# Cross attention in a transformer decoder: the shared table applied to four heads at once, and layer norm rows scaled by ScalarE

## The chip, the cores and the metric

The kernel runs on one core of one Trainium2 chip. The metric is device time in microseconds, from the start to the end of one execution; less is better. A core has five engines that run side by side, each with its own queue of instructions: PE (TensorE, matrix multiplications), DVE (VectorE), ACT (ScalarE), POOL (GpSimd) and SP (SyncE, which here issues DMA transfers). They wait for each other on semaphores.

## The reference

A two-layer decoder on x of 8 batches, 512 rows (positions) and 256 columns. Layer 0 has a self attention, a cross attention with 16 heads and a local transformer; layer 1 an integer attention, a media attention and a mixture of experts. The change lies in layer 0's cross attention and in the layer norms just before and behind it. Cut to what matters:

```python
def _layernorm(x, axis=-1, eps=1e-05):
    m = jnp.mean(x, axis=axis, keepdims=True)
    v = jnp.var(x, axis=axis, keepdims=True)
    return (x - m) / jnp.sqrt(v + eps)
...
        scores = scores + adj[None, None, :, :]
        scores = jnp.where(mask == 0, jnp.float32(-jnp.inf), scores)
        weights = jax.nn.softmax(scores, axis=-1)
```

The queries come from the layer norm of x, the keys and values from a context of 512 rows for each batch. `adj` is one table of 512x512 for all batches and heads, `mask` one of 512x512 for each batch and all heads. The result of the cross attention is added to x; the local transformer starts from the layer norm of the sum.

## The kernel before, in words

Everything here is float32. `FastDecoder` runs the stages one after the other; x lies in SBUF as 8 batches of 4 tiles of 128 rows by 256 columns.

**Table.** Since exp(s + a) = exp(s)·exp(a), the kernel takes the exponential of `adj` once, and for each batch multiplies it by (mask != 0) into `x_share` (L1608: four tiles of 128 keys by 512 queries). A step then needs the exponential of the scores times a tile of that table.

**Steps.** The stage's loop has 128 steps, 16 for each batch: four groups of four heads, each over four tiles of 128 keys. Step n does three things:
- `scores(n)`: four matmuls on four row groups of PE (L1720), which write two PSUM tiles `sc` of 128 x (2 heads x 512 queries), from a ring of three such tiles.
- `soften(n)`: for each of the two tiles an exponential on ACT into an SBUF tile `x_e` (L1731, ring of six), and a multiplication of it by the shared tile on DVE (L1732). The shared tile is broadcast over the two heads.
- `weigh(n-2)`: four matmuls that weigh the values with the multiplied exponentials of two steps before (L1748), summed over the four key tiles in one PSUM bank `po`. After the fourth key tile ACT copies `po` to `x_o` (L1754). Sums, a DMA, a reciprocal on DVE (L3248) and a multiplication on POOL (L1765) follow.

PE's order in a step is scores(n), weigh(n-2), then the extra matmuls.

**Work spread between the steps.** While one batch is in its 16 steps, `prepare` makes the next one's operands, a few pieces for each step: the keys (PE L1638, evacuated by ACT into `x_k`, L1653), `x_xn`, the normalised rows of x (L1614, through `normalize`, a DVE instruction for each tile of 128x256, L157), transposes (L1630, ACT L1633), queries (L1638 again, ACT `x_q` L1646), values (L1658, ACT `x_v` L1662), the table (L1608), and on POOL the addition of a bias to x once `x_xn` has been taken (L1619). These matmuls share one PSUM bank, `pj`, which ACT or DVE must have emptied before the next writes it.

The batch that ended before is finished in the same steps through a list `later` with delays in steps: output projections (PE L1781) and their addition to x on DVE (L1786) with the statistics for the next layer norm (L1491, L1492), a DMA that saves x to `away` (L1793), an estimate of the reciprocal root (L1495 to L1497) with three Newton rounds (L1502 to L1504) one step apart, and, from the fifth step on, the scaling of the four tiles of x in place, two to a step (`normal`, L1507, through `normalize`, L157; in the profile these are `x<-x,lt_ln_mean,lt_ln_rstd`).

**What sets the order.** A scheduler lays out each engine's queue by the program's order and priorities, and adds the semaphores. `paced` (L1703) puts a piece behind DVE's multiplication of the step before last, kept in `marks`; it only orders, and waits for nothing else. The mean and reciprocal root for `x_xn` of all batches are worked out in the self attention before, by `means` (L1419), and copied to `x_ln_mean` and `x_ln_rstd`; the first batch is prepared there too. In the last 12 steps the local transformer's first matmuls (L1885) are drawn in between.

Of the kernel before, what the change touches and what calls it, by code (L numbers as in the profile page):

```python
# [27 lines left out]
F32 = mybir.dt.float32  # L28
# [5 lines left out]
AF = mybir.ActivationFunctionType  # L34
ALU = mybir.AluOpType
# [4 lines left out]
P = 128  # L40
B, S, C = 8, 512, 256
NST = S // P
NT = B * NST
# [1234 lines left out]
class FastDecoder(Decoder):  # L1278
# [31 lines left out]
    def stage_self_attention(self, w, ahead):  # L1310
# [3 lines left out]
        nc = self.nc  # L1314
# [3 lines left out]
        with self.tc.tile_pool(reuse_waits="tile", name="sa", bufs=2) as pool, self.tc.tile_pool(  # L1318
# [4 lines left out]
            shift = self.alloc(pool, [P, 1], F32, "sa_shift", bufs=1)  # L1323
# [24 lines left out]
            def norm(b):  # L1348
                d = held[b] = {"h": hs[b % 2]}
                x = self.x[:, b * NST : (b + 1) * NST, :]  # L1350
                stats = self.ln_stats(pool, lambda i: [x[:, i, :]], NST, "sa_ln")
                d["xn"] = self.alloc(pool, [P, NST, C], F32, "sa_xn", bufs=3)
                for i in range(NST):
                    self.normalize(d["xn"][:, i, :], x[:, i, :], stats, i)
# [64 lines left out]
            def means(b):  # L1419

                x = self.x[:, b * NST : (b + 1) * NST, :]
                at = slice(b * NST, (b + 1) * NST)
                for kept, new in zip(self.x_ln, self.ln_stats(pool, lambda i: [x[:, i, :]], NST, "x_ln")):
                    nc.vector.tensor_copy(kept[:, at], new)

            self.x_ln = [self.alloc(self.const, [P, NT], F32, "x_ln_" + n) for n in ("mean", "rstd")]
            norm(0)
            norm(1)
            weights()
# [3 lines left out]
            for b in range(B):  # L1433
                scores(b)
                if b + 1 < B:
                    turn(b + 1)
                    project(b + 1)
                    values(b + 1)
                weigh(b)
                if b + 2 < B:  # L1440
                    norm(b + 2)
                if b > 0:
                    means(b - 1)
                    ahead.step(3)
# [24 lines left out]
    def rsqrt(self, pool, out, v, tag):  # L1469
# [4 lines left out]
        for _ in range(3):  # L1474
            nc.vector.scalar_tensor_tensor(t, out, -0.5, out, ALU.mult, ALU.mult)  # L1475
            nc.vector.tensor_tensor(t, t, v, ALU.mult)
            nc.vector.scalar_tensor_tensor(out, t, 1.5, out, ALU.add, ALU.mult)

    def ln_pieces(self, pool, rows, out, tag):


        nc = self.nc
        mv = self.alloc(pool, [P, NST, 2], F32, tag + "_mv")
        mean = self.alloc(pool, [P, NST], F32, tag + "_mean")
        var = self.alloc(pool, [P, NST], F32, tag + "_var")
        rstd = self.alloc(pool, [P, NST], F32, tag + "_rstd")
        t = self.alloc(pool, [P, NST], F32, tag + "_t")

        def stats(i):
            st = self.alloc(pool, [P, 1, 6], F32, tag + "_bn", bufs=4)  # L1490
            nc.vector.bn_stats(st[:, 0, :], rows[:, i, :])  # L1491
            nc.vector.bn_aggr(mv[:, i, :], st.rearrange("p a b -> p (a b)"))  # L1492

        def guess():
            nc.vector.tensor_copy(mean, mv[:, :, 0])  # L1495
            nc.vector.tensor_scalar(var, mv[:, :, 1], EPS, None, ALU.add)
            nc.vector.tensor_scalar(  # L1497
                rstd.bitcast(I32), var.bitcast(I32), -0.5, float(0x5F3759DF), ALU.mult, ALU.add
            )

        def newton():
            nc.vector.scalar_tensor_tensor(t, rstd, -0.5, rstd, ALU.mult, ALU.mult)  # L1502
            nc.vector.tensor_tensor(t, t, var, ALU.mult)
            nc.vector.scalar_tensor_tensor(rstd, t, 1.5, rstd, ALU.add, ALU.mult)  # L1504

        def normal(i):
            self.normalize(out(i), rows[:, i, :], (mean, rstd), i)  # L1507

        return (
            [lambda i=i: stats(i) for i in range(NST)], [guess] + [newton] * 3,  # L1510
            [lambda i=i: normal(i) for i in range(NST)],
        )

# [10 lines left out]
    def stage_cross_attention(self, ahead):  # L1524
# [6 lines left out]
        nc, t = self.nc, self.t  # L1531
# [7 lines left out]
        pool = first  # L1539
# [33 lines left out]
        bias = self.alloc(pool, [P, C], F32, "x_bias", bufs=1)  # L1573
# [14 lines left out]
        def prepare(b):  # L1588

            d = held[b] = {"v": v_pad[b % 2]}  # L1590
# [14 lines left out]
            def share(k):  # L1605
# [5 lines left out]

            x = self.x[:, b * NST : (b + 1) * NST, :]
            normals = [
                lambda i=i: self.normalize(d["xn"][:, i, :], x[:, i, :], self.x_ln, b * NST + i)  # L1614
                for i in range(NST)
            ]

# [75 lines left out]
        with self.tc.tile_pool(reuse_waits="tile", name="xa", bufs=2) as pool, self.tc.tile_pool(  # L1693
# [7 lines left out]
            marks = []  # L1701

            def paced(thunk):  # L1703

                with self.tc.issue_after(marks[-2]):
                    thunk()

            def scores(n):
# [16 lines left out]
            def soften(n):  # L1725
                b, rest = divmod(n, 16)
                kt = rest % 4
                d = held[b]
                for p in range(2):
                    ex = self.alloc(pool, [P, 2, 512], F32, "x_e", bufs=6)  # L1730
                    nc.scalar.activation(ex, d["e"][rest][p], AF.Exp)  # L1731
                    nc.vector.tensor_tensor(  # L1732
                        ex, ex, d["share"][:, kt, :].unsqueeze(1).broadcast_to([P, 2, 512]), ALU.mult
                    )
                    d["e"][rest][p] = ex
                marks.append(self.newest(mybir.EngineType.DVE))

            def weigh(n):
                b, rest = divmod(n, 16)
                G, kt = divmod(rest, 4)  # L1740
                g, e = divmod(G, 2)
                d = held[b]
                if kt == 0:
                    d["po"] = self.alloc(psum, [P, 512], F32, "po")
                ex = d["e"].pop(rest)
                for m in self.together(4):
                    r = (m + 2) % 4
                    nc.tensor.matmul(  # L1748
                        d["po"][32 * r : 32 * r + 32, :], d["v"][:, kt, 8 * g + 2 * r + e, :],
                        ex[r // 2][:, r % 2, :], start=(kt == 0), stop=(kt == 3),  # L1750
                    )
                if kt == 3:
                    o = self.alloc(pool, [P, S], F32, "x_o", bufs=3)
                    nc.scalar.copy(o, d["po"])  # L1754

                    if e == 0:
                        d["oT", g] = self.alloc(pool, [P, S], F32, "x_oT", bufs=5)
                        d["wide", g] = self.alloc(pool, [P, S], F32, "x_wide")
                    oT, wide = d["oT", g], d["wide", g]
                    at = [slice(32 * r + 16 * e, 32 * r + 16 * e + 16) for r in range(4)]  # L1760
                    for r in range(4):
                        nc.sync.dma_start(oT[at[r], :], o[32 * r + 1 : 32 * r + 17, :])

                    def multiply():
                        nc.gpsimd.tensor_tensor(oT, oT, wide, ALU.mult)  # L1765
                        if g == 1:
                            for i in range(NST):
                                later.add(3 + i, lambda i=i: project_out(b, i))

                    def divide(rows):  # L1770
                        for r in range(4):
                            nc.sync.dma_start(wide[at[r], :], rows[r : r + 1, :].broadcast_to([16, S]))
                        if e == 1:
                            later.add(2, multiply)

                    self.inverted(pool, o[0:P:32, :], later, divide)

            def project_out(b, i):
                ps = self.pj()
                for g in range(2):  # L1780
                    nc.tensor.matmul(  # L1781
                        ps[:, :C], held[b]["oT", g][:, i * P : (i + 1) * P], wo[:, g, :],
                        start=(g == 0), stop=(g == 1),
                    )
                x = self.x[:, b * NST + i, :]
                nc.vector.tensor_tensor(x, x, ps[:, :C], ALU.add)  # L1786
                if i == 0:
                    rows = self.x[:, b * NST : (b + 1) * NST, :]
                    held[b]["norm"] = self.ln_pieces(pool, rows, lambda i: rows[:, i, :], "lt_ln")
                means, roots, normals = held[b]["norm"]  # L1790
                means[i]()
                if i == NST - 1:
                    nc.sync.dma_start(self.away[b], self.x[:, b * NST : (b + 1) * NST, :])  # L1793
                    for k, root in enumerate(roots):
                        later.add(1 + k, lambda root=root: paced(root))
                    for k, normal in enumerate(normals):
                        later.add(5 + k // 2, lambda normal=normal: paced(normal))

            n = 16 * B
# [1719 lines left out]
```

## Time and profile before

| | |
|---|---|
| median of 3 runs | 3094.61 us (3087.45 to 3096.63) |
| profiled execution | 3094.66 us |
| its span, first to last instruction | 3092.7 us |
| mean granted TensorE clock | 0.974 |
| PE busy in the span | 2842.4 us (92%) |
| DVE busy | 2158.3 us (70%) |
| ACT busy | 1155.1 us (37%) |
| POOL busy | 409.6 us (13%) |

The cross attention's steps run from about 205 to 664 us of the span. In the profile's rows, `L1732 DVE TENSOR_TENSOR x_e<-x_e,x_share 128x1024` is DVE's instruction of line 1732, its output and inputs, and the shape in partitions by elements; then come the count, the busy time in all and the mean in ns of one, and the idle time of the engine just before such instructions, with the one that ended it. In rows of the timeline the first two numbers are the start and the length in us. PEld is PE's loading of weights, which overlaps its matmuls. Busy times of a pipelined engine overlap a little from one instruction to the next: two multiplications of 1.2 us start 1.13 us apart.

### The profile page before, as it was taken

To read this page: it belongs to the slowest core of one execution; us is meant where nothing else is said; L and a number is where in the kernel's file an instruction comes from. 1 tells how busy PE (TensorE), PEld (TensorE's weight loads), DVE (VectorE), ACT (ScalarE), POOL (GpSimd) and SP (SyncE) were. 2 spreads that over 40 slices of the span, in tenths; PEclk is the share of its full clock that TensorE was granted. 3 is DMA by queue.
4 is the path that set the end of the run, shared out by engine and by line. 5 is a ranking of instruction groups with operands and counts; after the bars stand their busy time and mean duration, and the time that the engine had idled before them with its cause. 6 is when DMAs were issued, how large, how long until landed. Compare 5 with 4: busy or idle time off the path is not lost. (4 is left out here: it accounts for less than half of the span.)

```text
span 3092.7 us, 40203 instructions
## 1 busy us (share of the span) xinstructions
PE 2842.4 (92%) x14929; PEld 1507.6 (49%) x14944; DVE 2158.3 (70%) x4962; ACT 1155.1 (37%) x1623; POOL 409.6 (13%) x389
## 2 busy tenths in 40 slices
PE   8999999969999999999999999999786999997998
PEld 5653333225555556555555556555344334434665
DVE  7458999977887894357887898548788766665110
ACT  2237777724334321124344331115263443441111
POOL 1111111100001010000101111112111123231111
PEclk9999999989999999999999999999997999998999
DMA  7011212101001001001000012010332122223231
GB/s 242 1 35 50 71 49 70 36 19 56 15 15 29 15 24 36 0 1 43 22 15 22 22 38 69 14 41 28 125 122 76 52 93 83 90 69 96 98 139 61
DMA packets 130696, 168.74 MB, mean 55 GB/s; under 512 B 51760, under 2 KB 79665, under 8 KB 128442
## 3 DMA queue, kind: packets, MB, share of 16 engines
q1 hardware_dynamic: 126394, 154.48, 16.0%
q0 software_dynamic: 4096, 11.59, 1.0%
q8 instruction: 119, 1.95, 0.3%
q14 instruction: 87, 0.71, 0.1%
HBM read 113.12 MB, written 47.50 MB: 52 GB/s over the span
## 5 line engine op out<-in xcount | busy, mean ns | idle before, releaser
L1885 PE MATMUL pj<-w,la_hT 128*128 128x512 f32 x720 | 342.8, 615 | 32.7 <-DVE x L2062 16.3
L1732 DVE TENSOR_TENSOR x_e<-x_e,x_share 128x1024 f32<-128x1024 f32 x256 | 317.6, 1283 | 16.7 <-ACT x_e L1731 16.5
L1731 ACT ACTIVATE x_e<-sc 128x1024 f32<-128x1024 f32 x256 | 249.4, 1023 | 82.0 <-PE sc L1720 82.0
L1885 PEld LDWEIGHTS pj<-w,la_hT 128*128 128x128 f32 x720 | 131.7, 194 | 189.3 <-issue 118.1
L2007 ACT ACTIVATE la_e<-la_e 128x1024 f32<-128x1024 f32 (+1 forms) x128 | 121.1, 952 | 209.2 <-DVE la_e L2003 209.2
L2890 ACT ACTIVATE ma_e<-sc,ma_bias 128x1024 f32<-128x1024 f32 x128 | 135.8, 1110 | 165.3 <-PE sc L2884 165.3
L2216 ACT ACTIVATE lf_gate<-pj,lf_b 128x512 f32<-128x512 f32 (+1 forms) x82 | 56.3, 687 | 346.6 <-PE pj L2195 337.2
L2897 DVE TENSOR_TENSOR ma_esum<-ma_esum,ma_e 128x1024 f32<-128x1024 f32 x96 | 129.8, 1353 | 71.3 <-ACT ma_e L2890 34.8
L2195 PE MATMUL pj<-lf_hnT,w 128*128 128x512 f32 (+1 forms) x368 | 171.7, 595 | 0.6 <-DVE lf_hid L2221 0.6
L2003 DVE TENSOR_TENSOR la_e<-sc,la_mask 128x1024 f32<-128x1024 f32 (+1 forms) x128 | 137.0, 1081 | 41.1 <-PE sc L1995 41.0
L3262 POOL TENSOR_TENSOR la_oT<-la_o,x_wide 128x512 f32<-128x512 f32 x64 | 88.3, 1387 | 571.0 <-DMA x_wide<-invs 315.4
L1748 PE MATMUL po<-x_e,x_v 128*32 128x512 f32 x1024 | 138.1, 612 | 21.9 <-DVE x_e L1732 15.2
L2195 PE MATMUL sc<-lf_hnT,w 128*128 128x512 f32 x336 | 157.9, 592 | 0.0
L1720 PE MATMUL sc<-x_q,x_k 32*128 32x512 f32 x1024 | 151.3, 640 | 1.7 <-DVE sa_ok L1448 1.4
L2267 PE MATMUL po<-w,lf_hid 128*128 128x256 f32 x640 | 148.8, 379 | 0.0
L2221 DVE SCALAR_TENSOR_TENSOR lf_hid<-sc,lf_b,lf_gate 128x512 f32<-128x512 f32 x70 | 52.4, 748 | 126.9 <-PE sc L2195 126.9
L1995 PE MATMUL sc<-la_qkT 64*128 64x256 f32 (+1 forms) x1024 | 124.2, 373 | 12.3 <-ACT la_qkT L1931 11.3
L1892 ACT ACTIVATE la_sq<-pj 128x512 f32<-128x512 f32 x120 | 71.4, 595 | 170.3 <-PE pj L1885 170.3
L2057 PE MATMUL pj<-w,la_oT 128*128 128x256 f32 x512 | 122.3, 385 | 11.3 <-DVE x L2062 9.4
L2884 PE MATMUL sc<-ma_qT,ma_kT 64*128 64x512 f32 x512 | 129.9, 626 | 0.0
L2267 PEld LDWEIGHTS po<-w,lf_hid 128*128 128x128 f32 x640 | 117.8, 190 | 20.2 <-issue 6.7
L2908 PE MATMUL po<-ma_e,ma_v 128*64 128x512 f32 x512 | 124.2, 606 | 0.0
(493 smaller groups left out, 5296.2 us busy)
## 6 DMA issues: line engine op xcount, KB each, us to landing
x_wide<-invs SPq DMA_DIRECT2D x184, 128.0 KB
w<-in_f_w_dram SPq DMA_DIRECT2D x16, 1024.0 KB
kv<-kv_o SPq DMA_DIRECT2D x56, 256.0 KB
slots<-x_empty SPq DMA_DIRECT2D x8, 1028.0 KB
x_mask<-in_x_maskT_dram SPq DMA_DIRECT2D x8, 1024.0 KB
ma_kT<-kv SPq DMA_DIRECT2D x8, 1024.0 KB
ma_v<-kv SPq DMA_DIRECT2D x8, 1024.0 KB
ex_rows<-slots SPq DMA_DIRECT2D x7, 1028.0 KB
```

Of the source, the lines that this page charges most:

```text
L1720: nc.tensor.matmul(pair[r // 2][:, r % 2, :], d["k"][rows, g, kt * P : (kt + 1) * P], d["q"][rows, e, g, :], start=True, stop=True,)
L1731: nc.scalar.activation(ex, d["e"][rest][p], AF.Exp)
L1732: nc.vector.tensor_tensor(ex, ex, d["share"][:, kt, :].unsqueeze(1).broadcast_to([P, 2, 512]), ALU.mult)
L1748: nc.tensor.matmul(d["po"][32 * r : 32 * r + 32, :], d["v"][:, kt, 8 * g + 2 * r + e, :], ex[r // 2][:, r % 2, :], start=(kt == 0), stop=( ...
L1885: nc.tensor.matmul(ps, d["hT"][:, k, i * P : (i + 1) * P], wqkv[:, k, j * S : (j + 1) * S], start=(k == 0), stop=(k == 1),)
L1995: nc.tensor.matmul(both[half][:, r, jj * 256 : jj * 256 + to - j * P], d["qkT"][rows, 4 + c, j * P : (j + 1) * P], d["qkT"][rows, c, j * P ...
L2003: nc.vector.tensor_tensor(ex[:, :, :n_cols], ps[:, :, :n_cols], mask[:, :n_cols].unsqueeze(1).broadcast_to([P, 2, n_cols]), ALU.add,)
L2195: nc.tensor.matmul(ps[:m, :], w1[:, k, at : at + m], held[b]["hnT"][:, k, :], start=(k == 0), stop=(k == 1))
L2267: nc.tensor.matmul(ps[:, :C], held[b]["hid"][:, f, i * P : (i + 1) * P], w2[:, f, :], start=(f == 0), stop=False,)
L2884: nc.tensor.matmul(both[m // 2][:, r, :], d["k"][rows, c, kt * P : (kt + 1) * P], d["q"][rows, c, :], start=True, stop=True,)
L2890: nc.scalar.activation(ex, ps, AF.Exp, bias=bias[:, b * NST + kt : b * NST + kt + 1], scale=0.125)
L2897: nc.vector.tensor_tensor(d["sum", c], d["sum", c], ex, ALU.add)
```

## The change

Three edits.

1. `soften` takes one tile `x_e` of 128 x (4 heads x 512), from a ring of three, in place of two of half the size from a ring of six. The two exponentials write its halves, and one multiplication of 128x2048 by the shared tile, broadcast over four heads, follows both. `weigh` reads the four heads from it. `marks` keeps the newest DVE and the newest ACT instruction of each step, and `paced` puts its piece behind both.
2. The scaling of rows goes from `normalize` (DVE, `(x - mean) * rstd`) to `on_scalar`, an ACT activation of kind Identity with a bias and a scale for each row: `x * rstd + shift`. That holds for `x_xn` (32 tiles over all batches) and for the rows of x behind the cross attention (32 tiles).
3. The shift, -mean·rstd, is made by DVE: in `means` by an instruction that takes the place of a copy, and in `ln_pieces` by one more 128x4 instruction in the last Newton round (`last`), once for each batch.

```diff
@@ means, in the self attention
-                for kept, new in zip(self.x_ln, self.ln_stats(pool, lambda i: [x[:, i, :]], NST, "x_ln")):
-                    nc.vector.tensor_copy(kept[:, at], new)
+                mean, rstd = self.ln_stats(pool, lambda i: [x[:, i, :]], NST, "x_ln")
+                shift, scale = self.x_ln
+                nc.vector.scalar_tensor_tensor(shift[:, at], mean, -1.0, rstd, ALU.mult, ALU.mult)
+                nc.vector.tensor_copy(scale[:, at], rstd)
@@
+    def on_scalar(self, out, in_, stats, i):
+        shift, scale = stats
+        self.nc.scalar.activation(
+            out, in_, AF.Identity, bias=shift[:, i : i + 1], scale=scale[:, i : i + 1]
+        )
@@ ln_pieces
+        def last():
+            newton()
+            nc.vector.scalar_tensor_tensor(mean, mean, -1.0, rstd, ALU.mult, ALU.mult)
+
         def normal(i):
-            self.normalize(out(i), rows[:, i, :], (mean, rstd), i)
+            self.on_scalar(out(i), rows[:, i, :], (mean, rstd), i)
...
-            [lambda i=i: stats(i) for i in range(NST)], [guess] + [newton] * 3,
+            [lambda i=i: stats(i) for i in range(NST)], [guess, newton, newton, last],
@@ prepare
-                lambda i=i: self.normalize(d["xn"][:, i, :], x[:, i, :], self.x_ln, b * NST + i)
+                lambda i=i: self.on_scalar(d["xn"][:, i, :], x[:, i, :], self.x_ln, b * NST + i)
@@ paced
-                with self.tc.issue_after(marks[-2]):
+                with self.tc.issue_after(marks[-2][0]), self.tc.issue_after(marks[-2][1]):
@@ soften
+                ex = self.alloc(pool, [P, 4, 512], F32, "x_e", bufs=3)
                 for p in range(2):
-                    ex = self.alloc(pool, [P, 2, 512], F32, "x_e", bufs=6)
-                    nc.scalar.activation(ex, d["e"][rest][p], AF.Exp)
-                    nc.vector.tensor_tensor(
-                        ex, ex, d["share"][:, kt, :].unsqueeze(1).broadcast_to([P, 2, 512]), ALU.mult
-                    )
-                    d["e"][rest][p] = ex
-                marks.append(self.newest(mybir.EngineType.DVE))
+                    nc.scalar.activation(ex[:, 2 * p : 2 * p + 2, :], d["e"][rest][p], AF.Exp)
+                nc.vector.tensor_tensor(
+                    ex, ex, d["share"][:, kt, :].unsqueeze(1).broadcast_to([P, 4, 512]), ALU.mult
+                )
+                d["e"][rest] = ex
+                marks.append([self.newest(e) for e in (mybir.EngineType.DVE, mybir.EngineType.Activation)])
@@ weigh
-                        ex[r // 2][:, r % 2, :], start=(kt == 0), stop=(kt == 3),
+                        ex[:, r, :], start=(kt == 0), stop=(kt == 3),
```

## The prediction, made before the result was known

> **What bounds the kernel now.** I read the costliest groups first, then busy time in a window, then the waits, then the timeline of one batch. Groups:
>
> ```profile
> L1732 DVE TENSOR_TENSOR x_e<-x_e,x_share 128x1024 f32<-128x1024 f32 x256 | 317.6, 1283 | 16.7 <-ACT x_e L1731 16.5
> L1731 ACT ACTIVATE x_e<-sc 128x1024 f32<-128x1024 f32 x256 | 249.4, 1023 | 82.0 <-PE sc L1720 82.0
> ```
>
> The multiplication is VectorE's dearest group and was let wait only 16.7 us. Windows (length, then PE, PEld, DVE, ACT, POOL busy, clock, DMA, GB/s): one whole batch, then the stage:
>
> ```profile
> 416.00:470.00 54.00, 51.21 (x313) 17.11 (x312) 51.06 (x73) 39.58 (x50) 8.11 (x3) 1.00 0.21 61
> 205.00:664.00 459.00, 417.06 (x2473) 135.13 (x2469) 420.83 (x601) 317.37 (x389) 56.71 (x27) 0.97 0.17 48
> ```
>
> A batch repeats every 53.9 us. PE and DVE are both 95% busy; ACT has a quarter free. Who waits for whom, over the stage (total, times, longest):
>
> ```profile
> PEld po L1748 <- DVE x_e L1732: 37.6, 42, 2.0
> PE po L1748 <- DVE x_e L1732: 15.2, 17, 3.7
> ```
>
> PE itself lost only 15.2 us to the multiplication (in most of the weight loads' 37.6 PE was still busy with the matmuls before). PE's own sum for a batch, from starts in the timeline: scores 1.07 + weighing 1.00, 16 times, 33.1; keys and queries 4x1.92 = 7.7; values 4x1.06; transposes 2x0.58; output projections 4x1.06; together 50.5. So 3.4 us of 53.9 is stall: **PE's issue order bounds the stage, and DVE is just behind it.** The two stretches of timeline where that decides, ACT, then DVE (start, length, what, idle before):
>
> ```profile
> 428.82 1.94 ACT L1731 ACTIVATE x_e<-sc 128x1024 f32<-128x1024 f32 x2 [0.44 <-PE sc L1720]
> 432.47 0.69 ACT L1653 ACTIVATE x_k<-pj,x_bk 128x512 f32<-128x512 f32 x1 [1.70 <-PE pj L1638]
> 433.57 1.94 ACT L1731 ACTIVATE x_e<-sc 128x1024 f32<-128x1024 f32 x2 [0.41 <-PE sc L1720]
> ```
>
> ```profile
> 429.68 2.35 DVE L1732 TENSOR_TENSOR x_e<-x_e,x_share 128x1024 f32<-128x1024 f32 x2
> 431.95 0.15 DVE L1502 SCALAR_TENSOR_TENSOR lt_ln_t<-lt_ln_rstd 128x4 f32<-128x4 f32 x1
> 432.14 0.16 DVE L1503 TENSOR_TENSOR lt_ln_t<-lt_ln_t,lt_ln_var 128x4 f32<-128x4 f32 x1
> 432.34 0.16 DVE L1504 SCALAR_TENSOR_TENSOR lt_ln_rstd<-lt_ln_t,lt_ln_rstd 128x4 f32<-128x4 f32 x1
> 432.42 2.35 DVE L1732 TENSOR_TENSOR x_e<-x_e,x_share 128x1024 f32<-128x1024 f32 x2
> 434.69 0.73 DVE L157 TENSOR_SCALAR x<-x,lt_ln_mean,lt_ln_rstd 128x256 f32<-128x256 f32 x2
> ```
>
> The exponentials from 428.82 are step 34's, the multiplication of step 34 starts at 432.42: DVE lags ACT by a whole step, and the last Newton round, which the row scaling needs, ends at 432.42.
>
> **The Trainium skill.** "VectorE: DVE Perf Modes", section "The TRN2 errata — SBUF-src ops pay a fixed extra latency per instruction": an fp32 two-tensor operation costs (N+151)/0.96 ns: 1224 at 1024, 691 at 512; the trace's median is 1216 (la_r, 128x512: 685), so it agrees. "ScalarE: Activation LUTs", section "What ACT_TABLE_LOAD costs": 186+0.833N ns with immediates, some 93 more for each [128,1] pointer operand, 93 of overlap back to back: 799 for x_q (512, two pointers), measured 773; near enough. "SBUF — State Buffer", section "SBUF: two separate sides": a two-tensor DVE operation and a GpSimd one lock each other out for a whole instruction; the mean 1283 over the median 1216, up to 3409, fits. "PSUM — Partial Sum Buffer", section "Engine vs sequencer instructions": an engine's queue is strictly first in, first out.
>
> **The change, part by part.**
>
> *Wide multiplication.* By extrapolation 1216 + 2x(1216-685) = 2278 ns (page: 2291). Starts show two halves 2.27 apart back to back with what follows; one wide costs about 2.2: 0.07 us of DVE pitch a step, 9 us over 128. Against it, the first half may start only when the second exponential is done, 1.0 us later, but a step's weights are used two steps later. In light steps (2.27 us apart) exponentials ending at 425.40 plus 2.3 give 427.7, and the weighing two steps on would come at about 427.68: no slack, no gain. I book nothing: the scores and extra matmuls that PE issues between hide it, and 0.2 us a light step (one without key, query or value matmuls; about 6 a batch, 7 batches, +8) is the cost if that cover is gone.
>
> *Removed from DVE.* 28 L157 at 612 ns (16.0 us) and 24 at 406 (8.8), 24.8 us in the stage window. They stood after the multiplications of steps 35 to 38, where PE, bound by keys and values, didn't wait. Gain on the path: 0. Eight extra 128x4 operations at 0.16 us: 1.3 us, 0.17 of it ahead of the scaling each time.
>
> *Added to ACT.* A 128x256 activation with two pointers isn't in the trace. Nearest: 773 - 256x0.833 = 560 ns (page, estimate: 585), pitch 0.46; bounds 0.40 (x_v, 403, no pointers) and 0.65. 64 x 0.46 = 30 us of ACT, which has 14 us a batch free. Work isn't the question, place is: by ACT's program order the first two scalings of lt rows stand between step 34's two exponentials. The last Newton round stands in DVE's queue after step 33's multiplication. The first exponential of step 34 ends about 429.84; the shift is ready at 432.42 + 0.17 = 432.6 less a little wide-multiply gain, say 432.45. ACT waits 2.6 us there, and queued behind it are the exponential, the key evacuation (so pj), and all later steps. From 432.45 ACT is one chain to the next po evacuation: four pairs of scalings at 0.93 (3.7), seven exponentials at 0.94 (6.6), two x_k at 0.6 (1.2), x_o 0.5: 12.0. The weighing of step 36, which needs po, starts at 444.6 to 444.7, where before:
>
> ```profile
> 442.81 1.06 PE L1748 MATMUL po<-x_e,x_v 128*32 128x512 f32 x8
> ```
>
> That is 1.9 us late, and the rest of the batch is PE's own work, which recovers nothing. The same DVE rows stand at 324.15 and 485.61 in other batches. Five batches have both lt rows and preparation: +9.5. Two have only the x_xn scalings, half an exponential pair each: +0.45, +0.9. The sixth lt batch, beside no preparation, stalled already for 1.76 before weighing at 601.14: +0.1. In sum +10.5.
>
> *Self-attention.* The first four x_xn scalings stand on ACT between exponentials of the second image; they wait for rstd and shift (ready about 50.4), and exponentials due at 48.65 and 50.37 and the copy of sa_xnT (50.95) queue behind, so the projection at 51.58 comes some 2.2 later: +2.2.
>
> *Tail of the stage, 601 to 664.* PE waits 10.13 and 4.18 us for DVE's la_v copies, which queue behind multiplications that now come whole, later by about 0.85 each: +1.8 (0 to 3).
>
> *Start of the local layers.* The last normals waited on DVE for the saving DMA, which landed at 704.27 (idle 4.83). Now ACT waits for it, with la_sq and la_qk behind it in its queue, where DVE had nothing pressing: +1.5 (0 to 2).
>
> POOL's bias addition (L1619) waited 42.3 us for x_xn from DVE and will wait for ACT instead, a little later; its reader is the output projection's addition to x more than twenty steps on, so 0. SP's and POOL's orders don't move; no DMA is added, but x's normals now reach SP's saving transfer from another engine: it reads x before they write, so it isn't later. Sum 10.5 + 2.2 + 1.8 + 1.5 = 16. The profiled execution took 3094.66 (span 3092.7, 2 outside), level with the median 3094.61: **3110 us**.
>
> **Rivals.**
>
> *B, covered.* ACT's wait is swallowed by PE's slack (sc has three buffers, weights two steps) and by the 3.4 us of stalls: about 3095. For: a quarter of ACT is free. Against: 12.0 us of unbroken chain after the wait.
>
> *C, faster.* DVE's relief ends its one-step lag. PE's waits for DVE at steps 30 to 34 (0.95 and 0.69 us in this batch) and 0.33 later vanish: 1.6x6 + 0.33x7 = 12, so about 3083. All that PE lost to DVE here, 15.2 (x_e) + 4.1 (lt_ln_t) + 3.5 (x L1786) = 23, bounds it at 3072. It decides if the shift is ready before step 34's first exponential ends, 2.6 us sooner than now. Against: the lag is made by a DMA wait (reciprocal at 424.10, idle 0.81) and by added rows before the scalings' place, and neither changes.
>
> *D, slower still.* As forecast, and the wide multiplication has no slack in light steps (+8), with GpSimd locking it out as a whole near L1619 (5 us, +3): about 3121.
>
> **How the numbers follow.** Chances: forecast 0.46, B 0.16, C 0.22, D 0.16. What a measurement of this kernel can tell from no change is about 0.3%, 9.3 us: below 3085.3 is faster, above 3103.9 slower. The forecast's own range is 3104 to 3118 (activation at 0.40 or 0.65: 8 scalings x 5 batches x up to 0.15 is 6 either way, tail and start 3). C straddles 3085 and D is wholly slower, so faster 0.20, same 0.18, slower 0.62. The range from 3084 to 3121 leaves out half of C and half of D.
>
> **What the profile after would show.** Right: 128 rows of 128x2048 at about 2.28; 64 ACT rows 128x256 at about 0.56; before the first lt scaling of each batch ACT idle about 2.6 us, released by DVE; a batch at about 55.8 us where both kinds stand, and PE's waits for ACT grown. Wrong: ACT idle there under 1 us and a batch at 52 to 53 (C), a batch at 53.9 (B), a multiplication at 2.4 or more with PE waiting for it in light steps (D). What would undo the forecast is DVE being ahead at step 33, so that nothing in ACT's queue waits, or an activation far from 0.56.

## The result: slower by 1%, and where the time went

The changed kernel took 3124.87 us (median of 4 runs, 3118.12 to 3126.87) against 3091.31 us for the kernel before beside it (4 runs, 3087.45 to 3096.63): a ratio of 1.0099, 95% interval 1.008 to 1.0118. The forecast was slower, 3110 us, at most 3121: the sign and the main mechanism were right, the size too small by almost half. The profiled execution has a span of 3120.8 us, 28.1 more than before.

Groups of the page after:

```profile
L1744 DVE TENSOR_TENSOR x_e<-x_e,x_share 128x2048 f32<-128x2048 f32 x128 | 304.6, 2394 | 68.4 <-ACT x_e L1743 68.4
L1743 ACT ACTIVATE x_e<-sc 128x1024 f32<-128x1024 f32 x256 | 250.0, 1024 | 71.5 <-PE sc L1732 66.2
```

DVE spends 13 us less on the multiplication (317.6 before) and idles 68.4 us before it for ACT, where it was 16.7. Busy time in the same two windows as before (length; PE, PEld, DVE, ACT, POOL; clock, DMA, GB/s):

```profile
416.00:470.00 54.00, 49.78 (x309) 16.11 (x302) 45.46 (x49) 40.99 (x55) 6.09 (x3) 1.00 0.19 60
205.00:664.00 459.00, 408.77 (x2401) 130.07 (x2399) 372.94 (x409) 329.20 (x428) 54.20 (x27) 0.97 0.16 47
```

DVE is relieved as meant, but by less than the 420.8 and 372.9 us of the window say, because the last four of the 128 steps now lie behind it: from the start of step 0 to that of step 127 DVE was busy for 409.8 us before and 378.2 after. PE, which sets the pace, did 2437 matmuls between these two starts in both kernels, in 445.5 us before and 464.9 after. The waits of the stage, 205 to 664 us (who, for whom: total, times, longest):

```profile
DVE x_e L1744 <- ACT x_e L1743: 63.4, 47, 4.5
PEld po L1760 <- DVE x_e L1744: 36.2, 27, 4.0
PEld po L1760 <- ACT x_o L1766: 20.9, 19, 1.4
PE po L1760 <- DVE x_e L1744: 20.4, 15, 3.7
ACT x L1483 <- DVE lt_ln_mean L1516: 12.3, 5, 2.8
```

The last row is the new wait that the forecast named: five times, up to 2.8 us. Where the span's 28.1 us arose is read from the starts of the first exponential of each step (ACT's rows are complete), after less before, and further on from the first lf_gate activation (of the local transformer's feed-forward part, at 1125 us before; la_ names belong to its attention):

| stretch | forecast, us | measured, us |
|---|---|---|
| up to step 0 (self attention) | 2.2 | 1.75 |
| steps 0 to 32 | 0.9 | 1.85 |
| steps 32 to 112 (five batches with lt scalings and preparation) | 9.5 | 16.2 |
| steps 112 to 127 (sixth lt batch and tail) | 1.9 | 1.45 |
| step 127 to the first lf_gate | 1.5 | 7.6 |
| the rest | 0 | -0.65 |
| sum | 16 | 28.1 |

**One of the five batches, as the timeline has it after** (ACT, DVE, POOL and PE, each asked by itself; start, length, what, idle before). It is the batch shown before, with its step 64 now 9.63 us later:

```profile
438.19 1.02 ACT L1743 ACTIVATE x_e<-sc 128x1024 f32<-128x1024 f32 x1 [0.45 <-PE sc L1732]
442.05 1.09 ACT L1483 ACTIVATE x<-x,lt_ln_mean,lt_ln_rstd 128x256 f32<-128x256 f32 x2 [2.83 <-DVE lt_ln_mean L1516]
443.05 1.00 ACT L1743 ACTIVATE x_e<-sc 128x1024 f32<-128x1024 f32 x1
```

```profile
441.81 0.16 DVE L1516 SCALAR_TENSOR_TENSOR lt_ln_mean<-lt_ln_mean,lt_ln_rstd 128x4 f32<-128x4 f32 x1
444.08 2.29 DVE L1744 TENSOR_TENSOR x_e<-x_e,x_share 128x2048 f32<-128x2048 f32 x1 [2.11 <-ACT x_e L1743]
...
453.68 6.68 DVE L1744 TENSOR_TENSOR x_e<-x_e,x_share 128x2048 f32<-128x2048 f32 x2 [1.12 <-ACT x_e L1743]
```

```profile
453.64 2.36 POOL L1631 TENSOR_TENSOR x<-x,x_bias 128x1024 f32<-128x1024 f32 x1
```

```profile
454.17 1.07 PE L1760 MATMUL po<-x_e,x_v 128*32 128x512 f32 x8 [0.35 <-ACT x_o L1766]
...
458.21 1.06 PE L1760 MATMUL po<-x_e,x_v 128*32 128x512 f32 x8 [0.84 <-DVE x_e L1744]
```

The two scalings stand between the exponentials of 438.19 and 443.05, which are one step's. ACT idles 2.83 us, then DVE idles 2.11 us, because the wide multiplication needs the second exponential. The weighing that needs po starts at 454.17; it was 442.81, so less the 9.63 it is 1.73 late: the 1.9 of the forecast. (The prediction calls the steps of this batch's scalings 34 to 38; by the count of the stage's 128 steps they are 66 to 70. Its sum doesn't rest on the number.) What the forecast lacked is the next weighing, which waited 0.84 us for DVE: two wide multiplications took 6.68 us where 4.5 is usual, while POOL's bias addition ran. Before, four halves took about as long, but DVE had started them in time (POOL, DVE):

```profile
445.39 5.05 POOL L1619 TENSOR_TENSOR x<-x,x_bias 128x1024 f32<-128x1024 f32 x1 [3.47 <-DVE x_xn L157]
```

```profile
448.27 6.66 DVE L1732 TENSOR_TENSOR x_e<-x_e,x_share 128x1024 f32<-128x1024 f32 x4
```

**Some three of the 28 us follow a late transfer.** Batch 5 (steps 80 to 96) alone lost 5.9 us, the other four between 1.9 and 3.1 (in a second profile of this kernel 4.9, and 2.7 to 4.1). In it the reciprocal of the sums waited 2.89 us for a DMA (0.50 before), PE waited 3.13, and then ran at half clock (window's columns as above; DVE, PE, then the window):

```profile
492.35 0.25 DVE L3260 RECIPROCAL x_inv<-x_sums 128x16 f32<-128x16 f32 x1 [2.89 <-DMA x_sums<-sums]
```

```profile
494.81 1.94 PE L1760 MATMUL po<-x_e,x_v 128*32 128x512 f32 x8 [3.13 <-DVE x_e L1744]
```

```profile
495.00:500.00 5.00, 5.00 (x24) 0.73 (x18) 4.90 (x8) 1.61 (x2) 0.00 (x0) 0.50 0.16 43
```

The eight matmuls took 1.94 us, 1.06 at full clock. The late transfer is not the change's alone: of five profiles of the kernel before, one (before_d, below) has a wait of 2.56 us for it too, and lost 2.2 us in that batch; the other four wait 0.26 to 0.50.

**The start of the local layers.** Not the scalings made it late: ACT's last ones waited only 0.23 us for the saving DMA, and wide_only (below), which has them on DVE, lost 9.4 us in this stretch. PE's clock did. Between step 127 and the first of the last eight output projections, half clock stood for 14.2 us where it was 6.8 before, and 3.6 us were lost; two groups of four matmuls took some 3.4 us each, 1.98 before. One of them, before and then after:

```profile
669.79 1.98 PE L1885 MATMUL pj<-w,la_hT 128*128 128x512 f32 x4 [0.68 <-ACT la_qkT L1931]
```

```profile
692.63 3.46 PE L1897 MATMUL pj<-w,la_hT 128*128 128x512 f32 x4 [0.68 <-ACT la_qkT L1943]
```

Then the eight projections ran at half clock. The second of them, before and then after:

```profile
683.21 1.13 PE L1781 MATMUL pj<-w,x_oT 128*128 128x256 f32 x4 [0.52 <-DVE x L1786]
```

```profile
708.99 2.08 PE L1793 MATMUL pj<-w,x_oT 128*128 128x256 f32 x4 [0.52 <-DVE x L1798]
```

From one to the next it is 2.59 us, where it was 1.64, with the same 0.5 us of idle between them. Only the last interval was no shorter before (2.67). Over the seven intervals that is 5.6 us; 1.6 came back up to the first lf_gate, which leaves 7.6.

### The profile page after: what moved, and what is told of

Its sections match the earlier page's. It is cut to its first block, busy times and chain, and to the rows that moved or that the text cites. A ratio compares the mean times of both kernels' runs of the same rounds, so it can differ in the third digit from the quotient of the medians.

```text
span 3120.8 us, 40054 instructions
## 1 busy us (share of the span) xinstructions
PE 2858.3 (92%) x14929; PEld 1511.3 (48%) x14944; DVE 2125.1 (68%) x4778; ACT 1183.3 (38%) x1687; POOL 409.0 (13%) x389
## 5 line engine op out<-in xcount | busy, mean ns | idle before, releaser
L1744 DVE TENSOR_TENSOR x_e<-x_e,x_share 128x2048 f32<-128x2048 f32 x128 | 304.6, 2394 | 68.4 <-ACT x_e L1743 68.4
L2069 PE MATMUL pj<-w,la_oT 128*128 128x256 f32 x512 | 122.3, 385 | 12.1 <-DVE x L2074 10.2
```

The lines of the kernel that those rows point to most:

```text
L1744: nc.vector.tensor_tensor(ex, ex, d["share"][:, kt, :].unsqueeze(1).broadcast_to([P, 4, 512]), ALU.mult)
```

## Experiments

"By step 127" means the start of the stage's last step, against the first profile of the kernel before (650.85 us there; 647.7 to 650.9 over five profiles of it, so that the reference is the latest of the five). What two profiles of one kernel differ by at this point says what a few us can mean: 0.2 us for wide_only, 0.6 for the changed kernel, 4.0 for scalar_only. Times are against the kernel before beside them; its medians in the three timed sessions were 3096.4, 3095.9 and 3094.1 us.

**First round: the parts alone, and the wait alone.**

```diff
@@ wide_only
-                nc.vector.scalar_tensor_tensor(shift[:, at], mean, -1.0, rstd, ALU.mult, ALU.mult)
+                nc.vector.tensor_copy(shift[:, at], mean)
@@ wide_only, lt_dve
-            self.on_scalar(out(i), rows[:, i, :], (mean, rstd), i)
+            self.normalize(out(i), rows[:, i, :], (mean, rstd), i)
...
-            [lambda i=i: stats(i) for i in range(NST)], [guess, newton, newton, last],
+            [lambda i=i: stats(i) for i in range(NST)], [guess, newton, newton, newton],
@@ wide_only
-                lambda i=i: self.on_scalar(d["xn"][:, i, :], x[:, i, :], self.x_ln, b * NST + i)
+                lambda i=i: self.normalize(d["xn"][:, i, :], x[:, i, :], self.x_ln, b * NST + i)
@@ lt_later
-                        later.add(5 + k // 2, lambda normal=normal: paced(normal))
+                        later.add(6 + k // 2, lambda normal=normal: paced(normal))
```

scalar_only has `soften` and `weigh` as before, but for `marks`, and all else as changed.

> The wide multiplication alone; both kinds of row scaling and the mean stay on DVE as before. Theory P (place: ACT's queue waits for DVE's shift, and the scalings stand between a step's two exponentials): the wide multiplication by itself costs little, 3090 to 3097 us, with the 16 steps of batches 2 to 6 at 53 to 54 us. Rival M (the wide multiplication, starting only after both exponentials and locked by GpSimd as a whole, is the larger part): 3105 us or more, 55 us a batch.

> Both kinds of row scaling on ACT, the multiplication in two halves as before. Theory P: nearly all of the loss is here, 3112 to 3125 us, and ACT still idles about 2.8 us before the first lt scaling of a batch. Rival M: less than half of the loss is here, 3095 to 3105 us.

> The changed kernel with the lt scalings one step later (delay 6 in place of 5), so that they stand behind the second exponential of the step in which the shift is made. Theory P: ACT's idle time before them, 12.3 us in the stage, falls under 2 us, and a batch with both kinds gets some 1.9 us shorter: 3122 - 5 x 1.9 = 3113 us. Rival W (it is ACT's added work in these steps that delays, wherever its wait is): 3120 us or more.

> The changed kernel with the lt scalings back on DVE, x_xn on ACT, wide multiplication. Theory P: the batches lose the 1.9 us of the wait, but the loss seen in the batches with x_xn alone (about 1.3 us at their steps 6 to 9) stays in seven batches, and self attention's 1.75 us: 3091 + 9 + 2 = 3102 us. Rival M: 3110 us or more.

| run | median, us | ratio, 95% interval | later by step 127, us | DVE idle for ACT, us |
|---|---|---|---|---|
| changed kernel | 3124.87 | 1.0099, 1.008 to 1.0118 | 21.2 | 63.4 |
| wide_only | 3108.49 | 1.0046, 1.0028 to 1.0064 | 2.9 | 29.6 |
| scalar_only | 3099.69 | 1.0013, 1.0 to 1.0025 | 2.8 | 34.3 |
| lt_later | 3118.26 | 1.0065, 1.0047 to 1.0084 | 12.1 | 57.8 |
| lt_dve | 3111.4 | 1.005, 1.0033 to 1.0067 | 9.5 | 51.0 |

Both theories miss. The scalings alone cost 0.13%, not nearly all, as theory P had it. Rival M's times come true in wide_only, scalar_only and lt_dve (3111.4 us, forecast 3110 or more), but its reason doesn't: the wide multiplication alone cost 0.46%, yet not where M had it: from step 32 to 80, three batches, it lost 0.1 us, and 9.4 of its 12.3 us up to the first lf_gate lie behind step 127. In the stage **2.9 and 2.8 us make 21.2 together**; in a second profile of each, 3.1 and 6.8 make 21.9. So the sum of the parts is uncertain, 6 to 10 us (1.7 of it lost in the self attention), but well below the whole. scalar_only shows why. ACT there (timeline):

```profile
375.56 1.94 ACT L1743 ACTIVATE x_e<-sc 128x1024 f32<-128x1024 f32 x2 [0.44 <-PE sc L1732]
379.52 1.09 ACT L1483 ACTIVATE x<-x,lt_ln_mean,lt_ln_rstd 128x256 f32<-128x256 f32 x2 [2.03 <-issue]
380.52 0.67 ACT L1665 ACTIVATE x_k<-pj,x_bk 128x512 f32<-128x512 f32 x1
```

and DVE:

```profile
379.27 0.16 DVE L1516 SCALAR_TENSOR_TENSOR lt_ln_mean<-lt_ln_mean,lt_ln_rstd 128x4 f32<-128x4 f32 x1
379.36 2.35 DVE L1744 TENSOR_TENSOR x_e<-x_e,x_share 128x1024 f32<-128x1024 f32 x2
```

ACT waits 2.03 us here too, but with multiplications in halves the scheduler has put the scalings behind both exponentials of the step, and DVE finds its work done: both halves follow the shift without idle time, where the changed kernel has 2.11 us. The scalings' place differs so throughout: of the 52 scalings from step 0 to step 127, the changed kernel has all 52 between the two exponentials of a step, scalar_only none. lt_later takes the wait away (ACT's 12.3 us for lt_ln_mean become 0.4) and leaves 42 of the 52 between the exponentials: from step 32 to 80 it lost 4.3 us, where the changed kernel lost 8.4 (10.5 in its second profile), so the wait is worth 1.4 to 2 us a batch; the forecast had 1.9. Its time, 3118.26 us, lies between theory P's 3113 and rival W's 3120. lt_dve, with x_xn alone between the exponentials, lost 1.8 in the same stretch.

**Second round: is it the scaling between a step's exponentials?**

```diff
@@ pair_kept and pair_later, in soften
-    for p in range(2):
-        nc.scalar.activation(ex[:, 2 * p : 2 * p + 2, :], d["e"][rest][p], AF.Exp)
+    nc.scalar.activation(ex[:, :2, :], d["e"][rest][0], AF.Exp)
+    first_exp = self.newest(mybir.EngineType.Activation)
+    with self.tc.issue_after(first_exp), self.tc.high_priority(self.AT_ONCE):
+        nc.scalar.activation(ex[:, 2:, :], d["e"][rest][1], AF.Exp)
@@ pair_later
-    later.add(5 + k // 2, lambda normal=normal: paced(normal))
+    later.add(6 + k // 2, lambda normal=normal: paced(normal))
```

> The changed kernel with the two exponentials of a step tied together in ACT's queue, so that no scaling stands between them; all else as changed. The wide multiplication alone cost 2.9 us by step 127 of the stage, the scalings alone 2.8, both together 21.2. Theory I (the interaction: in the changed kernel the scalings stand between a step's two exponentials, and the wide multiplication needs both): with the pair tied the parts add up, some 6 us by step 127, and DVE's idle time for ACT in the stage falls from 63 us to 40 or less; 3106 to 3112 us. Rival W (ACT's wait and work in these steps matter wherever they stand): 15 us or more by step 127, 3118 us or more.

> As pair_kept, and the lt scalings one step later, so that ACT doesn't wait for the shift either. Theory I: what is left of the wait, 0 to 1 us a batch, goes: 3 to 6 us by step 127, at most 4 us faster than pair_kept. Rival W: 5 us or more faster than pair_kept.

DVE's waits for ACT in the stage, in pair_kept and then in its opposite of the first round, lt_later (total, times, longest):

```profile
DVE x_e L1746 <- ACT x_e L1745: 43.5, 43, 3.9
```

```profile
DVE x_e L1744 <- ACT x_e L1743: 57.8, 45, 4.2
```

pair_kept was 6.8 us late by step 127 (forecast 6) and DVE idled 43.5 us for ACT (forecast 40 or less, missed); 3105.71 us, ratio 1.0028 (1.0013 to 1.0042). pair_later: 6.3 us, 45.9 us, 3105.89 us, ratio 1.0032 (1.002 to 1.0043). None of the 52 scalings stands between a step's exponentials in either. With the pair tied, 14 of the 21 us go, and taking the wait for the shift away changes nothing more that could be told apart (0.5 us by step 127, 0.2 in the median). That is what theory I says; rival W, 15 us or more, is out. Tying the pair moves other instructions too: the copies to x_q stand elsewhere among the exponentials, and pair_kept stood at 9.4 us at step 112 and got 2.7 back in the tail, so it is no clean undoing of one thing.

So I made twins which have every scaling at the same place in ACT's order and differ in the multiplication. (One thing more moves with it: in each batch one copy to x_v stands between two exponentials in the split twin and behind both in the wide one.) In both, the scalings wait in a list; `soften` issues them behind its first exponential, and its second one behind them. The x_xn scalings go into the list two groups of `prepare` earlier than before.

```diff
+    if p == 0 and waiting:
+        with self.tc.issue_after(self.newest(mybir.EngineType.Activation)):
+            while waiting:
+                waiting.pop(0)()
+        last_act = self.newest(mybir.EngineType.Activation)
...
-    yield [normals[0], normals[1], V[0]]
+    yield [V[0]]
...
-    later.add(5 + k // 2, lambda normal=normal: paced(normal))
+    later.add(4 + k // 2, lambda normal=normal: waiting.append(normal))
```

Both leave out the scaling of the last two batches' eight tiles of x, which comes behind the start of the stage's last step; what is compared lies ahead of it.

> Scalings on ACT, multiplication in two halves, and the scalings (x_xn first, then lt, four at a time) forced between the two exponentials of steps 4 and 5 of a batch, later than the changed kernel has them, so that ACT doesn't wait for the shift. Its twin wide_between has the same order on ACT with one wide multiplication. Theory I (what costs is a scaling between the exponentials together with a multiplication that needs both): 2 to 6 us by step 127. Rival W (a scaling between the exponentials costs by itself, since the second score tile and its buffer are held): 10 us or more by step 127.

> The twin of split_between with the wide multiplication. Theory I: 9 us or more by step 127, at least 5 more than split_between. Rival W: within 3 us of split_between.

| later by, us | step 16 | step 32 | step 80 | step 127 |
|---|---|---|---|---|
| split_between | 1.2 | 0.0 | 4.4 | 10.5 |
| wide_between | 2.6 | 4.0 | 9.9 | 16.5 |

The wide twin lost 6.0 us more (theory I: at least 5; rival W: within 3), but the split one lost 10.5, more than theory I allows (2 to 6) and as much as rival W said (10 or more). Of that, 5.6 us lie in batch 5, which lost time in all the changed forms and in one of five profiles of the kernel before; the three lt batches ahead cost it 1.5 us each. So neither theory is the whole: a scaling between the exponentials costs something with either multiplication, and the wide one adds to it. By how much is less sure than 6.0 looks: each twin has one profile, and scalar_only's two, of one program, are 4.0 us apart. Times: 3099.33 (1.0019, 1.0008 to 1.0031) and 3116.5 us (1.0082, 1.0065 to 1.0099). Of these 17 us, some 8 lie between step 127 and the first lf_gate, where the wide twin ran at half clock and the split one didn't (see the half clock at the projections, below).

**Is DVE's relief worth anything?**

```diff
                 lambda i=i: self.on_scalar(d["xn"][:, i, :], x[:, i, :], self.x_ln, b * NST + i)
+                if b
+                else nc.vector.tensor_scalar(
+                    d["xn"][:, i, :], x[:, i, :], self.x_ln[1][:, i : i + 1], self.x_ln[0][:, i : i + 1],
+                    ALU.mult, ALU.add,
+                )
```

xn_scalar has this, the multiplication in halves, and the lt scalings on DVE as in lt_dve.

> The multiplication in halves, lt scalings and the first batch's x_xn on DVE, x_xn of batches 1 to 7 on ACT behind both exponentials: the part of the change that relieves DVE of its dearest scalings and makes ACT wait for nothing. If PE bounds the stage, the relief buys next to nothing: step 127 within 2 us of before, 3092 to 3099 us. If DVE bounds it (rival C of the prediction), some 28 x 0.5 us come off in part: step 127 4 us earlier or more.

3094.2 us, ratio 1.0002 (0.999 to 1.0015), 0.9 us earlier by step 127. DVE's busy time from 205 to 664 us fell from 420.8 to 410.4 and nothing came of it that the spread of the kernel before doesn't cover: a relief of this size isn't what the stage lacks, and rival C of the prediction falls. No form beat the kernel before.

**The half clock at the projections.**

> The kernel before once more, for its clock at the start of the local layers. In its first profile PE had the full clock from 664 to 694 us, in the profiles of all five changed forms it had half the clock for 24 to 41 us in that stretch. If that half clock comes with the change, this profile shows the full clock again and a span near 3092; if it comes and goes from run to run, and explains the spread of 3086 to 3105 us of the kernel before, it can show the half clock here, with a span of 3100 or more.

> The changed kernel once more: step 127 within 3 us of its first profile (672.1 us), since the order of the queues is the same; half clock at the start of the local layers again, 20 us or more, if it comes with the change.

> The kernel before a third time, for PE's clock between 664 and 694 us. Seven profiles of changed forms and one repeat had the half clock there for 24 us or more, two of before none. If it comes with the later end of the stage, this one shows the full clock again; if it is chance, it has one in two of showing the half clock.

> The kernel before a fourth time. Theory L (the half clock while the last output projections run depends on where the sparse matmuls ahead of them fall in the throttle's slices of some 3.4 us, and the kernel before happens to fall well): full clock at the projections again, 1.64 us from one to the next. Rival R (chance of each execution): 2.59 us from one to the next in about one of two.

> The kernel before a fifth time. Theory L: 1.64 us from one projection to the next. Rival R: 2.59 us in about one of two.

> The scalings alone, once more. Theory L: 2.59 us from one projection to the next, as in its first profile. Rival R: 1.64 us in about one of two.

> The wide multiplication alone, once more. Theory L: 2.59 us from one projection to the next. Rival R: 1.64 us in about one of two.

The changed kernel's second profile repeats the first: 21.9 us by step 127, half clock at the projections (2.59 us). Of the kernel before, before_a, before_b and before_c ran them 1.64 us apart and before_d 2.59 (2.13 the first time); scalar_only did 2.59 in its first profile, scalar_only_b 1.64; wide_only_b 2.59, as wide_only. So the clock there is not fixed by the kernel: theory L falls. Nor is it even chance: all nine profiles of forms with the wide multiplication ran at half clock there, of nine without it two did (before_d, scalar_only). Why the wide form meets it so often isn't shown; so it stays open whether these us are a cost of the wide multiplication or of what its order brings to PE at that moment. PE's work ahead of the projections is the same in both: besides full matmuls, groups of transposes of 0.66 us with 0.68 us of waiting between. The Trainium skill, "TensorE: Matmul & The Clock Gate", section "What's actually happening", has the throttle judge PE's activity in windows of 3413 ns that run freely and don't start with the kernel, and section "Part 4: PE-mode transpose" says that transposes don't count as busy in the same way. The clock's records here change in steps of 3.41 us, and the same kernel fell on either side in repeats, which agrees with the first; the second no run here tells apart. I could not make out a threshold from the records. The kernel before spread from 3085 to 3107 us over some 100 runs, and part of that lies in such stretches elsewhere: before_a ended 6.4 us later than the first profile, with step 127 at the same time and 30 us more at half clock.

## Why the prediction was wrong in size

The forecast had 16 us and the profile 28.1, 12.1 more. 7.6 of these lie in steps 0 to 112, of them some 3 in batch 5's late transfer, and 6.1 between step 127 and the first lf_gate; the other terms came out 1.6 smaller. So two terms were mis-sized: the nothing for the wide multiplication, and the 1.5 us for the start of the local layers.

*ACT waits for the shift, with the exponential behind it.* Right, and well sized in its place: forecast ACT idle about 2.6 us, released by DVE, in five batches, measured 2.83 in the batch shown; activation 0.56 us, chain to the weighing 1.9 us late and a batch of 55.8 us, measured 0.594, 1.73 and 56.4 in the batch shown (56.9 in the one before it). The Trainium skill's rule of the queue (strictly first in, first out), "PSUM — Partial Sum Buffer", section "Engine vs sequencer instructions", was the one that carried it, and the trace agrees: the exponential of 443.05 stands behind the scalings that waited 2.83 us. My estimate from "ScalarE: Activation LUTs", section "What ACT_TABLE_LOAD costs", 585 ns, was nearer to the measured 594 than the 560 that I took from the trace.

*"I book nothing" for the wide multiplication.* This step failed. It was argued for each part by itself, and by itself it was right: wide_only lost 0.1 us over three batches, and the multiplication took its 2.29 us. But the cover named, the scores and extra matmuls that PE issues in the two steps between a multiplication and its weighing, is the same cover that ACT's wait uses up. With ACT late, the multiplication couldn't start on the first half while the scalings held the second, and the bias addition then met a late DVE (0.84 us in the batch shown). 9.5 + 0.9 us were forecast for steps 0 to 112, 18.0 measured, of them some 3 in batch 5. Tying the two exponentials, so that no scaling stands between them, brought the loss by step 127 from 21.2 us to 6.8. The bias addition stood in rival D, as a mishap apart; it belonged in the forecast's own sum. A smaller gap goes with it: the prediction priced the wait of the first scalings between two exponentials, and not the further scalings between them; split_between, where ACT never waits for the shift, lost 1.5 us in each of the three lt batches ahead of the late transfer.

*Batch 5's late transfer* was in no case of the prediction. The same reciprocal waited 2.77 us in wide_only and 2.23 in scalar_only; in the kernel before 0.26 to 0.50 in four profiles, but 2.56 in before_d. So most changed forms meet it, and the unchanged kernel can. What delays the transfer was not tried.

*Self attention*: 2.2 forecast, 1.75 measured, by the mechanism named (ACT idle 2.93 us before the first x_xn scaling, released by DVE's x_ln_rstd). lt_dve, scalar_only and both pair runs show the same 1.6 to 1.75 us; wide_only shows none.

*Tail*: 1.9 with the sixth batch, measured 1.45; PE's longest wait for the la_v copies grew from 10.13 to 11.5 us.

*Start of the local layers*: 1.5 forecast, 7.6 measured. The step failed in its cause, not its size alone. The wait for the saving DMA is nearly gone (0.23 us); PE's clock took the time, 3.6 us ahead of the last projections and 5.6 in them. Half clock stood in the prediction nowhere, although the profile before showed it (10 us from 629 us on, beside PE's wait of 10.13).

*The rivals.* B, covered, and C, faster, are out, C also by xn_scalar. D came nearest, with 3121, but that is luck in part: it put 8 us on light steps and 3 on POOL's bias addition, and wide_only, which has both, lost 0.1 us over three batches. Of D's two causes only the second is seen in the changed kernel, and there because ACT was late; the clock and batch 5's transfer, some 9 of the 12 us by which the forecast fell short, were in neither D nor the forecast.

## What to carry to other kernels

Two edits that are each nearly free may use the same slack; ask what covers an edit, and whether the other edit has already spent it. When operations are merged so that one needs two producers, look at what a scheduler will put between the two: here a scaling of 0.6 us that itself waits for the merged engine. Moving work from a busy engine bought nothing here, where another engine's order set the pace, and moved waits into a queue that has other readers. And profile a form twice before reading a difference of a few microseconds.

## What the runs showed of the hardware

- A 128x2048 float32 multiplication on DVE took 2.28 to 2.29 us undisturbed, against two of 1.22 us; the mean over all was 2.39 in the changed kernel and 2.36 in wide_only.
- A 128x256 Identity with bias and scale for each row, SBUF to SBUF, took 583 to 600 ns on ACT, and two back to back 1.09 us.
- POOL's bias addition of 128x1024 took 2.36 us where it began 0.04 us ahead of a multiplication on DVE (the batch shown), and 5.05 us before, where it began while one was running; DVE's multiplications beside it took 2.1 to 2.2 us more in both. In the changed kernel five of the eight additions began so, 0.03 to 0.04 us ahead.
- Sparse matmuls kept the half clock for over 20 us: eight groups of four at 2.07 us with 0.5 us between them, 80% busy, while the same groups at full clock, 1.13 us with 0.5 between, 69% busy, kept the full one.
